# A graph's normalized input, turned by DMA in two 16-bit planes instead of by TensorE

## The chip, the core and the metric

The kernel runs on one core of one Trainium2 chip. The metric is the time of one execution on the device, in microseconds (us). The core has five engines that run side by side and wait for each other through semaphores: TensorE (PE, with its weight loads shown apart as PEld), VectorE (DVE), ScalarE (ACT), GpSimd (POOL) and SyncE (SP), which here only issues DMAs. Each engine works through its own queue in order. Matrix results land in PSUM[...]; everything else lives in SBUF, 128 partitions wide.

## The reference

There are 64 graphs of 256 nodes with 512 features each (`x` is 64 x 256 x 512, fp32) and an adjacency of 256 x 256 booleans for each. Two layers follow one another, and each adds its result to `x`:

```python
h = jnp.maximum(_layernorm(x, axis=-1), 0.0)
x = x + _L0_gnn_ref(h, adj, ...)   # 8 heads of 64
h = jnp.maximum(_layernorm(x, axis=-1), 0.0)
x = x + _L1_gnn_ref(h, adj, ...)   # 4 heads of 64
```

Layer 0 maps `h` with one matrix to `m`, takes queries and keys from `m`, forms softmax scores over 256 nodes and keeps those edges whose cosine between the heads of `m` is over 0.1, then mixes messages (`h` through another matrix) with them. Layer 1 is a plain masked attention over `h`. What matters here is the first step of layer 0: `h` is the layer norm of `x` with a ReLU behind it, and the products need it with the features on the partitions, so the 256 x 512 matrix of a graph has to be turned.

## The kernel before

All matrices are fp32. The features of a graph lie in tiles `[128, 4, 256]` (128 features on the partitions, four groups of them, 256 nodes); the nodes-first form `xs` is `[128, 2, 512]`. The products with 512 x 512 matrices are done in seven block products instead of eight (`seven_products`, lines 245 to 310), whose left factors `ss` come from GpSimd (`left_factors`, tile `sh`, line 235). `seven_products` is a generator: every `next` on it issues one piece, so pieces of several products stand between each other in the program.

The order of every engine's instructions is the order of the program (`manual_schedule`). The loop is `period(i)`, run for i = 0 to 64 (line 541 on). In one period four graphs are worked on at different stages:

- `b` = graph i-1: the rest of its layer 1 (scores `sc1`, mask, sums `zb`, values, the product `p_o` with the result, the store);
- `g` = graph i: layer 0's scores `sc0`, cosines `co`, edge selection, values, and its layer-1 input and projections `p_qk`, `p_v`;
- `nx` = graph i+1: layer 0's map `p_m`, messages `p_s`, queries `p_q`, keys `p_k`, norms;
- `n2` = graph i+2: its moments (mean and variance by `bn_stats`), the deviation, the normalized rows `xn`, and the turned input `hT`.

Graph i+3 is loaded in the period (lines 183 and 185), after the store of `b`, in whose buffer it lands.

For n2, before the change: `moments` on VectorE in the middle of the period (lines 193 to 196), `deviations` with the Sqrt on ScalarE next to g's own (line 199), `normalized` on VectorE (line 206: subtract the mean, multiply by 1/deviation), and at the end of the period `normal_input`, which is `turned` and `left_factors`. `turned` (lines 210 to 217) transposes each 128 x 128 block with a TensorE matmul against the identity (line 215, four for each half, tile `p_t`, one PSUM bank for each half) and lets ScalarE apply the ReLU while it moves the bank to `hT` (line 216). The same helper turns g's layer-1 input, tile name `hT` too.

Three other things share resources with the change:

- ScalarE has to load a table of functions before Sqrt and before Exp. A period does this once each: all Sqrt instructions stand together (lines 199 and 637), and a dummy Exp on `spare` (line 639) brings the Exp table back before the next scores.
- SyncE issues all DMAs of the loop: the `far` transposes (line 439, four in a period, 16-bit, 128x256), the `mask` transposes (line 324), the spread of the softmax sums through DRAM (`by_rz` line 358, `own` line 360), the spread of the norms (`by_rn`, `nT`), the store (646) and the loads.
- Tiles of a pool with one buffer are reused by tag. `kT` is written by `keys(nx)` and read by the next period's `sc0`; `nT` is written by `spread(nx)` near the end of a period and last read by the next period's cosines; `hT` of nx is read by its map and messages.

Of the kernel before, what the change touches and what calls it, by code (L numbers as in the profile page):

```python
# [8 lines left out]
F32 = mybir.dt.float32  # L9
BF16 = mybir.dt.bfloat16  # L10
I32 = mybir.dt.int32
U8 = mybir.dt.uint8
AF = mybir.ActivationFunctionType
ALU = mybir.AluOpType
AX = mybir.AxisListType
# [131 lines left out]
def fast_path(ctx, tc, a, w, chk, out):  # L147
# [4 lines left out]
    nc = tc.nc  # L152
    x, adj = a["x"], a["adj"]
    B, S, D = x.shape
    P, DH = 128, 64
# [17 lines left out]
    def bank(name, shape=(P, 2, S), dtype=F32):  # L173
        return ring.tile(list(shape), dtype, tag="bank", name=name)
# [14 lines left out]
    def moments(g, tag):  # L189
        st = small.tile([P, NT, 6], F32, tag="st", name=f"st{tag}")  # L190
        g.mv = small.tile([P, NT, 2], F32, tag="mv", name=f"mv{tag}")
        for t in range(NT):
            nc.vector.bn_stats(st[:, t, :], g.xs[:, t, :])  # L193
            nc.vector.bn_aggr(g.mv[:, t, :], st[:, t, :])
        g.rs = small.tile([P, NT], F32, tag="rs", name=f"rs{tag}")
        nc.vector.tensor_scalar_add(g.rs, g.mv[:, :, 1], LN_EPS)

    def deviations(g):
        nc.scalar.activation(g.rs, g.rs, AF.Sqrt)
        nc.vector.reciprocal(g.rs, g.rs)  # L200

    def normalized(g, tag):
        g.xn = []
        for t in range(NT):
            xn = sb2.tile([P, D], F32, tag="xn", name=f"xn{tag}_{t}")
            nc.vector.tensor_scalar(xn, g.xs[:, t, :], g.mv[:, t, 0:1], g.rs[:, t:t + 1],  # L206
                                    op0=ALU.subtract, op1=ALU.mult)
            g.xn.append(xn)
# [7 lines left out]
            nc.scalar.activation(hT[:, :, t * P:(t + 1) * P], p, AF.Relu)  # L216
        return hT

    def features_first(wt, src, ms, name):

        p = bank(name)
        nk = wt.shape[1]
        for n, m in enumerate(ms):
            for c in range(nk):
                nc.tensor.matmul(p[:, n, :], wt[:, c, m * P:(m + 1) * P], src[:, c, :],
                                 start=(c == 0), stop=(c == nk - 1))
        return p

# [210 lines left out]
    def far_added(g, c):  # L441
        if not g.last:
            nc.gpsimd.tensor_add(g.d[c], g.d[c], g.e[c][:, :, :S])  # L443
# [97 lines left out]
    def period(i):  # L541
        g = graphs.get(i) if i < B else None
        b, nx, n2 = graphs.get(i - 1), graphs.get(i + 1), graphs.get(i + 2)
        def off_edges(cs):
            for c in cs if g else ():
                masked(g.e[c], g.mask, edges=False)
                g.d[c] = halves(g.e[c], f"0_{i}_{c}")


        if b:  # L550
            b.e1 = [exps(products(b.k1T, b.q1T, c, f"sc1_{b.i}_{c}"), f"1_{b.i}_{c}") for c in range(NIC)]
            for c in range(NIC):
                masked(b.e1[c], b.mask, edges=True)
            if b.last:
                for t in range(NT):
                    values_in(b, t)
            else:
                b.d1 = [halves(b.e1[c], f"1_{b.i}_{c}") for c in range(NIC)]
        if nx:
            m, s = mapped(nx), messages(nx)  # L560
            next(m)
        if g:
            for c in range(NKC):
                g.e[c] = exps(products(g.kT, g.qT, c, f"sc0_{i}_{c}"), f"0_{i}_{c}")
        if nx:
            next(s)
        off_edges((0, 1))
        if nx:
            next(m)
        off_edges((2,))  # L570
        if nx:
            next(m)
            next(s)
            next(m)
            halved(nx)

        if g:
            for c in range(NKC):
                far_off(g, c, cosines(g, c))
                if c == 0:  # L580
                    off_edges((3,))
            for c in range(NKC):
                far_added(g, c)
        if nx:
            q = queries(nx)
            next(q)
            next(s)
            next(q)
            squares(nx)
            next(s)  # L590
        for c in range(NKC):
            if g:
                far_back(g, c)
            if nx and c < 3:
                next((q, s, q)[c])
        if nx:
            lengths(nx, norms(nx))

        if i == 0:
            w.finish_seven(w.wqk1)  # L600
        if b:
            sums1(b)
            values1(b)
        if n2:
            moments(n2, f"0_{n2.i}")
        if g:
            g.avs = sb1.tile([P, NKC, S], F32, tag="wide", name=f"avs{i}")
            g.sms = sb1.tile([P, S], F32, tag="sms", name=f"sms{i}")
            values(g, 0)
            values(g, 1)  # L610
            sums(g)
        if nx:
            k = keys(nx)
            next(k)
        if b:
            nc.scalar.activation(b.rz, b.rz, AF.Copy, accum_out=chk[:, b.i, 3:4])
        if g:
            sums_back(g)
            heads_back(g)
        if nx:  # L620
            next(k)
        if n2:
            edges(n2)
        if b:
            divided(b)
        if g:
            moments(g, f"1_{i}")
        if nx:
            next(k)
        if g:  # L630
            deviations(g)
        if n2:
            deviations(n2)
        if g:
            normalized(g, f"1_{i}")
        if nx:
            nc.scalar.activation(nx.rn, nx.rn, AF.Sqrt)

        nc.scalar.activation(spare[:, 1:], spare[:, :1], AF.Exp)
        if b:  # L640
            for t in range(NT):
                result(b, t)
                if b.last:
                    nc.sync.dma_start(out=out_t[b.i][:, t], in_=b.xs[:, t])
            if not b.last:
                nc.sync.dma_start(out=out_t[b.i], in_=b.xs)
        if i + 3 < B:
            graphs[i + 3] = load(i + 3)
        if g:
            g.h1T = turned(g, f"1_{i}", "wide")  # L650
            j = queries_keys1(g)
            for t in range(NT):
                nc.gpsimd.tensor_add(g.xs[:, t, :], g.xs[:, t, :], w.bo_b)
        if nx:
            next(k)
        if g:
            next(j)
        if nx:
            nc.vector.reciprocal(nx.rn, nx.rn)
            spread(nx)  # L660
        if g:
            next(j)
        if n2:
            normalized(n2, f"0_{n2.i}")
        if g:
            next(j)
            if not g.last:
                values_in(g, 0)
            next(j)
        if n2:  # L670
            normal_input(n2)
        if g and not g.last:
            values_in(g, 1)
        if nx:
            units(nx)
# [5 lines left out]
    with tc.manual_schedule():  # L681
        spare = small.tile([P, 2], F32, tag="spare", name="spare", bufs=1)
        nc.vector.memset(spare, 0.0)
        graphs = {0: load(0)}
        w.load_map()
        gws = [sb2.tile([P, 2, D], F32, tag="e", name=f"gw{k}", bufs=6) for k in range(2)]
        w.load_folded(gws)
        w.load_scores()
        graphs.update({n: load(n) for n in range(1, min(3, B))})
        w.load_rest()  # L690

        def normal(n):
            moments(graphs[n], f"0_{n}")
            deviations(graphs[n])
            normalized(graphs[n], f"0_{n}")

        g = graphs[0]
        normal(0)
        normal_input(g)
        edges(g)  # L700
        w.finish_seven(w.wm)
        m = mapped(g)
        next(m)
        next(m)
        w.fold(gws, bank, w.put_seven)
        next(m)
        w.finish_seven(w.wq)
        next(m)
        halved(g)
        squares(g)  # L710
        w.finish_seven(w.wk)
        q, k, s = queries(g), keys(g), messages(g)
        next(q)
        lengths(g, norms(g))
        w.fold_bias(sb2.tile([P, NKC, P], F32, tag="xn", name="gbb"), bank)
        w.finish_seven(w.wc)
        for step in (k, q, k, q, k, q, k):
            next(step)
        nc.scalar.activation(g.rn, g.rn, AF.Sqrt)
        nc.vector.reciprocal(g.rn, g.rn)  # L720
        spread(g)
        if B > 1:
            edges(graphs[1])
            normal(1)
        nc.scalar.activation(spare[:, 1:], spare[:, :1], AF.Exp)
        for _ in range(5):
            next(s)
        units(g)
        if B > 1:
            normal_input(graphs[1])  # L730
        for i in range(B + 1):
            period(i)

# [297 lines left out]
```

## Time and profile before

| | |
|---|---|
| median of 3 runs | 3752.13 us (3750.98 to 3752.83) |
| span of the profiled execution | 3750.8 us |
| one period in the middle | about 57.5 us |
| p_t transposes on TensorE (line 215) | 1024, 272 to 448 ns each as shown, overlapping |
| ReLU evictions of p_t (line 216) | 256, 595 ns each |
| xn on VectorE (line 206) | 256, 929 ns each |
| bn_stats on VectorE (line 193) | 256, 666 ns each |
| far transposes (line 439) and mask transposes (line 324) | 256 and 128, 1.21 and 1.23 us of SyncE each |

How to read it: an instruction's duration on TensorE is longer than its place in the queue, since matmuls overlap. The chain of waits followed back from the last instruction gives the place: each piece of it begins where the one before ends. "Idle before" an instruction is the time in which its engine did nothing, with the instruction it waited for. Time of DMA-issuing instructions is not counted as busy.

### The profile page before, as it was taken

How to read it: one execution, taken by the hardware profiler on the slowest of the kernel's cores; microseconds unless marked ns; L12 is line 12 of the kernel's file. 1: busy time of each engine (PE TensorE's matmuls, PEld its weight loads, DVE VectorE, ACT ScalarE, POOL GpSimd, SP SyncE). 2: the span in 40 equal slices, each digit the busy share in tenths (PEclk: the TensorE clock that was granted, in tenths of full speed). 3: DMA queues.
4: the chain of work that ended last, by engine and by line, in shares of the span. 5: the costliest groups of instructions: out<-in, count | busy, mean ns of one | idle time of the engine just before them, and what ended most of it. 6: DMA issues, size and time to landing. Idle time of an engine off the chain costs nothing.

```text
span 3750.8 us, 76663 instructions
## 1 busy us (share of the span) xinstructions
PE 3704.9 (99%) x29649; PEld 3145.3 (84%) x29649; DVE 2878.5 (77%) x5350; ACT 1587.8 (42%) x4108; POOL 2468.6 (66%) x2044
## 2 busy tenths in 40 slices
PE   7999999999999999999999999999999999999997
PEld 7888888888888888888888888888888888888885
DVE  6777777777777777777777777777777777777775
ACT  2444444444444444444444444444444444444443
POOL 3667666676676676676766766767667667666673
PEclk9999999999999999999999999999999999999999
DMA  3111111111111111111111111111111111111101
GB/s 101 39 39 41 48 32 48 48 29 47 45 35 48 33 46 48 32 46 45 33 48 39 41 48 32 48 48 29 47 45 34 48 33 47 48 32 46 46 26 35
DMA packets 226096, 159.23 MB, mean 42 GB/s; under 512 B 137536, under 2 KB 192064, under 8 KB 225728
## 3 DMA queue, kind: packets, MB, share of 16 engines
q1 hardware_dynamic: 223456, 154.22, 14.4%
q8 instruction: 238, 3.90, 0.4%
q14 instruction: 130, 1.06, 0.1%
q10 hardware_dynamic: 2272, 0.04, 0.0%
HBM read 94.67 MB, written 34.34 MB: 34 GB/s over the span
## 4 chain that ended last, share of the span: by engine, by line
PE 97%; DVE 1%; DMA 1%; POOL 0%; issue 0%; SPq 0%; ACT 0%; DVEq 0%; ACTq 0%; POOLq 0%
PE sc L386 9%; PE av L413 9%; PE p_q L261 6%; PE p_m L261 6%; PE p_k L261 6%; PE p_qk L261 6%; PE p_s L256 6%; PE p_o L538 6%; PE p_v L505 6%; PE p_q_z L261 5%; PE co L423 5%; PE p_qk_z L261 5%; PE p_m_z L261 5%; PE p_k_z L261 4%; PE p_s_z L256 4%; PE p_t L215 3%
## 5 line engine op out<-in xcount | busy, mean ns | idle before, releaser
L406 POOL TENSOR_TENSOR d<-e 128x512 f32<-128x512 f32 x382 | 721.0, 1913 | 34.5 <-DVE e L400 28.9
L402 DVE TENSOR_TENSOR e<-e,mask 128x1024 f32<-128x1024 f32 x256 | 456.9, 1805 | 64.2 <-ACT e L393 64.2
L239 POOL TENSOR_TENSOR sh<-hT 128x256 f32<-128x256 f32 x128 | 93.0, 726 | 585.6 <-ACT hT L216 585.6
L393 ACT ACTIVATE e<-sc 128x512 f32<-128x512 f32 x768 | 389.8, 620 | 143.3 <-PE sc L386 143.1
L491 POOL TENSOR_TENSOR xs<-xs,o 128x512 f32<-128x512 f32 x128 | 187.4, 1484 | 387.2 <-DVE o L489 387.2
L450 POOL TENSOR_TENSOR d<-d,e 128x512 f32<-128x512 f32 x252 | 321.0, 1274 | 171.7 <-DVE e L448 169.9
L443 POOL TENSOR_TENSOR d<-d,e 128x512 f32<-128x512 f32 x252 | 311.8, 1267 | 0.0
L436 DVE SCALAR_TENSOR_TENSOR e<-co,e 128x256 f32<-128x256 f32 (+1 forms) x1024 | 282.1, 343 | 35.8 <-ACT up L433 34.7
L216 ACT ACTIVATE hT<-p_t 128x512 f32<-128x512 f32 x256 | 139.2, 595 | 280.8 <-PE p_t L215 280.8
L538 PE MATMUL p_o<-wo,own 128*128 128x512 f32 x512 | 234.9, 602 | 9.6 <-DVE own L533 9.6
L505 PE MATMUL p_v<-wv,hT 128*128 128x256 f32 x1024 | 242.1, 379 | 0.0
L386 PE MATMUL sc<-qT,kT 64*128 64x256 f32 x2048 | 238.2, 382 | 0.0
L433 ACT ACTIVATE up<-co,below 128x128 bf16<-128x128 f32 x512 | 159.6, 366 | 183.0 <-PE co L423 177.3
L413 PE MATMUL av<-e,sem 128*64 128x256 f32 x2048 | 232.2, 379 | 0.9 <-DVE e L448 0.9
L448 DVE SCALAR_TENSOR_TENSOR e<-far,e 128x256 f32<-128x256 bf16 x256 | 230.5, 901 | 0.0
L206 DVE TENSOR_SCALAR xn<-xs,mv,rs 128x512 f32<-128x512 f32 x256 | 227.4, 929 | 0.1
L386 PEld LDWEIGHTS sc<-qT,kT 64*128 64x128 f32 x2048 | 192.9, 187 | 27.5
L413 PEld LDWEIGHTS av<-e,sem 128*64 128x64 f32 x2048 | 146.8, 137 | 75.6 <-DVE e L448 1.7
L505 PEld LDWEIGHTS p_v<-wv,hT 128*128 128x128 f32 x1024 | 184.7, 190 | 20.2 <-issue 0.3
L400 DVE SCALAR_TENSOR_TENSOR e<-mask,e 128x1024 f32<-128x1024 bf16 x128 | 184.8, 1482 | 21.8 <-ACT e L393 21.8
L193 DVE BATCH_NORM_STATS2 st<-xs 128x6 f32<-128x512 f32 x256 | 170.6, 666 | 24.8 <-POOL xs L491 21.7
L423 PE MATMUL co<-nT 64*128 64x256 f32 (+1 forms) x2048 | 184.9, 330 | 0.0
(194 smaller groups left out, 9008.8 us busy)
## 6 DMA issues: line engine op xcount, KB each, us to landing
xs<-in_x_dram SPq DMA_DIRECT2D x64, 512.0 KB
nT<-by_rn SPq DMA_DIRECT2D x128, 256.0 KB
out_dram<-xs SPq DMA_DIRECT2D x63, 512.0 KB
own<-by_rz SPq DMA_DIRECT2D x128, 128.0 KB
ad<-in_adj_dram SPq DMA_DIRECT2D x64, 64.0 KB
far<-up SPq DMA_TRANSPOSE x256
mask<-adb SPq DMA_TRANSPOSE x128
wm<-in_L_gnn_map_w_dram SPq DMA_DIRECT2D x4, 256.0 KB
```

The source lines that it names most:

```text
L256: nc.tensor.matmul(region, src[:, c, :], wt[:, block, c, :], start=p not in opened, stop=True, skip_group_check=True)
L261: nc.tensor.matmul(region[:, f, :], wt[:, block, c, f * P:(f + 1) * P], src[:, c, :], start=p not in opened, stop=True, skip_group_check=True)
L386: nc.tensor.matmul(ps[s][:, j, :], rows[h, c, j * P:(j + 1) * P], cols[h, c, :], start=True, stop=True)
L393: nc.scalar.activation(e[:, s, :], p.rearrange("p j q -> p (j q)"), AF.Exp, scale=SCALE)
L402: nc.vector.tensor_mul(e, e, m)
L406: nc.gpsimd.tensor_add(d, e[:, :, :S], e[:, :, S:])
L413: nc.tensor.matmul(av[s * DH:(s + 1) * DH, n, :], vs[:, j, (h0 + s) * DH:(h0 + s + 1) * DH], q[:, s, j * S:(j + 1) * S], start=(j == 0), s ...
L423: nc.tensor.matmul(ps[s][:, j, j * P:], g.nT[h, c, j * P:(j + 1) * P], g.nT[h, c, j * P:], start=(j == 0), stop=True, skip_group_check=True)
L443: nc.gpsimd.tensor_add(g.d[c], g.d[c], g.e[c][:, :, :S])
L450: nc.gpsimd.tensor_add(g.d[c], g.d[c], g.e[c][:, :, S:])
L505: nc.tensor.matmul(g.p_v[:, t, :], g.h1T[:, c, t * P:(t + 1) * P], w.wv1[:, c, :], start=(c == 0), stop=(c == NKC - 1))
L538: nc.tensor.matmul(p, b.avs1[:, c, t * P:(t + 1) * P], w.wo1[:, c, :], start=(c == 0), stop=(c == NIC - 1))
```

## The change

For graphs 2 to 63 the input of layer 0 is no longer turned on TensorE. ScalarE normalizes it and applies the ReLU in one instruction (scale 1/deviation, bias -mean/deviation). The DMA transpose turns 16-bit elements, so each fp32 word is seen as two 16-bit halves: ScalarE copies the low halves and the high halves apart into `flat` (nodes first), SyncE issues a DMA transpose for each half and each half of the nodes into `turn`, and ScalarE puts the halves back together in `hT` (`join`, once for each plane).

```diff
+    def shifts(g, tag):
+
+        deviations(g)
+        g.shift = small.tile([P, NT], F32, tag="shift", name=f"shift{tag}")
+        nc.vector.scalar_tensor_tensor(g.shift, g.mv[:, :, 0], -1.0, g.rs, op0=ALU.mult, op1=ALU.mult)
+        g.flat = sb1.tile([P, NT, 2, D], U16, tag="kT", name=f"flat{tag}")
+        g.turn = sb1.tile([P, 2, NKC, S], U16, tag="nT", name=f"turn{tag}")
+
+    def sent(g, tag, t):
+
+        xn = sb2.tile([P, D], F32, tag="xn", name=f"xn{tag}_{t}")
+        nc.scalar.activation(xn, g.xs[:, t, :], AF.Relu, bias=g.shift[:, t:t + 1], scale=g.rs[:, t:t + 1])
+        bits = xn.bitcast(U16).rearrange("p (d k) -> p k d", k=2)
+        for k in range(2):
+            nc.scalar.copy(g.flat[:, t, k, :], bits[:, k, :])
+            nc.sync.dma_start_transpose(out=g.turn[:, k, :, t * P:(t + 1) * P], in_=g.flat[:, t, k, :])
+
+    def joined(g, tag):
+        g.hT = sb1.tile([P, NKC, S], F32, tag="hT", name=f"hT{tag}")
+        g.bits = g.hT.bitcast(U16).rearrange("p c (q k) -> p k c q", k=2)
+
+    def join(g, k):
+        nc.scalar.copy(g.bits[:, k], g.turn[:, k])
```

The pieces go into the period at these places (a helper `features_first` that nothing calls is dropped as well):

```diff
             for c in range(NKC):
                 far_added(g, c)
+        if n2:
+            shifts(n2, f"0_{n2.i}")
         if nx:
             q = queries(nx)
             next(q)
             next(s)
+        if n2:
+            sent(n2, f"0_{n2.i}", 0)
+        if nx:
             next(q)
             squares(nx)
             next(s)
+        if n2:
+            sent(n2, f"0_{n2.i}", 1)
...
-        if n2:
-            moments(n2, f"0_{n2.i}")
...
             sums(g)
+        if n2:
+            joined(n2, f"0_{n2.i}")
+            join(n2, 0)
...
             heads_back(g)
+        if n2:
+            join(n2, 1)
...
-        if n2:
-            deviations(n2)
...
-        if n2:
-            normalized(n2, f"0_{n2.i}")
...
         if n2:
-            normal_input(n2)
+            n2.left_h = left_factors(n2.hT, "sh", n2.i)
+        if i + 3 < B:
+            moments(graphs[i + 3], f"0_{i + 3}")
```

The moments are now taken one period earlier, at the end of the period in which the graph is loaded, since the deviation is needed in the middle of the next one; for graph 2 they are taken ahead of the loop. `flat` uses the buffer of `kT` and `turn` that of `nT`, in the part of the period in which those are not in use. Graphs 0 and 1 are still turned on TensorE ahead of the loop.

More of the change, by code (lines that the diff above doesn't have):

```diff
@@ L12 @@
 U8 = mybir.dt.uint8
+U16 = mybir.dt.uint16
 AF = mybir.ActivationFunctionType
@@ L217, in turned @@
         return hT
[L219 to L227, printed above, removed]
+    def shifts(g, tag):
[16 more added lines that the diff above has]
+        nc.scalar.copy(g.bits[:, k], g.turn[:, k])
     HC = NKC // 2
@@ L730, in fast_path @@
             normal_input(graphs[1])
+        if B > 2:
+            moments(graphs[2], "0_2")
         for i in range(B + 1):
```

## The prediction

> **What bounds the kernel now.** I first read the page's busy shares and the chain that ended last, to see which engine sets the end:
>
> ```profile
> PE 3704.9 (99%) x29649; PEld 3145.3 (84%) x29649; DVE 2878.5 (77%) x5350; ACT 1587.8 (42%) x4108; POOL 2468.6 (66%) x2044
> PE 97%; DVE 1%; DMA 1%; POOL 0%; issue 0%; SPq 0%; ACT 0%; DVEq 0%; ACTq 0%; POOLq 0%
> ```
>
> TensorE is busy 99% of the span, and 97% of the chain is TensorE work following TensorE work. So an instruction taken off TensorE shortens the kernel by its place in that chain, as long as nothing else becomes late. Next I read the chain in order of time through one period in the middle (pieces: start us, us, what), where the transposes stand:
>
> ```profile
> 1829.37 0.88 PE p_t L215 x8
> 1830.25 0.89 PE p_k_z L261 x8
> ...
> 1838.23 0.89 PE p_qk_z L261 x8
> 1839.12 0.87 PE p_t L215 x8
> 1839.99 1.73 PE p_v L505 x8
> ...
> 1886.83 0.87 PE p_t L215 x8
> ```
>
> There are two groups of eight transposes in a period. The first (1829.37) turns g's layer-1 input and stays; the second (1839.12, between the last p_qk_z and the second half of p_v) is `normal_input(n2)` and goes. It costs 0.87 us of unbroken chain. The period is 1886.83 - 1829.37 = 57.46 us, and its 50 pieces join without a hole, so TensorE has no idle time into which a late input could fall. Every new wait of TensorE therefore costs in full, and what matters is the slack of the other engines where the new work lands. ScalarE takes nearly all of it, so I read its timeline over a period (start, us, work, in brackets the idle time before):
>
> ```profile
> 1856.56 2.59 ACT L433 ACTIVATE up<-co,below 128x128 bf16<-128x128 f32 x8 [2.81 <-PE co L423]
> 1860.56 0.62 ACT L278 ACTIVATE u2p_q<-p_q,bq 128x128 f32<-128x128 f32 x2 [1.41 <-issue]
> ...
> 1865.84 0.62 ACT L278 ACTIVATE u5p_q<-p_q,bq 128x128 f32<-128x128 f32 x2 [4.14 <-PE p_q L261]
> 1866.36 1.15 ACT L334 ACTIVATE sq<-mT 128x512 f32<-128x512 f32 x2
> 1870.48 0.38 ACT L528 ACTIVATE rz<-zb 128x256 f32<-128x256 f32 x1 [2.97 <-PE zb L524]
> ...
> 1878.76 0.62 ACT L278 ACTIVATE u2p_k<-p_k,bk 128x128 f32<-128x128 f32 x2 [1.48 <-PE p_k L261]
> ...
> 1882.53 0.62 ACT L278 ACTIVATE u5p_k<-p_k,bk 128x128 f32<-128x128 f32 x2 [2.04 <-PE p_k L261]
> ```
>
> The holes of 1.41, 4.14, 2.97, 1.48 and 2.04 us are where the change puts its work. The new transfers go to the one queue of SyncE, so its timeline comes last:
>
> ```profile
> 1857.21 6.05 SPq L439 DMA_TRANSPOSE far<-up  x4
> 1874.98 0.56 SPq L358 DMA_DIRECT2D by_rz<-rz  x1
> 1876.69 1.25 SPq L360 DMA_DIRECT2D own<-by_rz  x2
> ```
>
> Between the end of the far transposes, 1863.26, and by_rz at 1874.98 the queue has 11.7 us free.
>
> **What the Trainium skill says.** "ScalarE: Activation LUTs", What ACT_TABLE_LOAD costs, prices an ACTIVATE at 186 ns + 0.833 ns per element, 93 ns more per [128,1] operand, 93 ns of overlap back to back; 512 elements come to 612 ns, and the trace's avs eviction of 128x512 takes 597, so I use it. The same section gives a table load 1283 ns, as the trace does (1283), and about 1380 ns of drain. The trace has no drain: a load starts at 1883.17 and the next ACTIVATE at 1884.51. Its section Table sets says that relu, copy and identity are in every set; the trace agrees, since in the prologue Relu, Identity, Copy and Square run between the Sqrt load at 5.44 and the Exp load at 52.81 with no load between. "DMA: Bandwidth & Descriptors", DMA Transpose (X-bar), allows 2-byte elements only, hence two planes, and wants transposes of two streams kept apart; here all are issued by SyncE, as far and mask are already.
>
> **The change part by part.**
> *Off TensorE*: eight transposes, 0.87 us, for graphs 2 to 63 (0 and 1 are still turned on TensorE): 62 x 0.87 = 53.9 us, on the path. *Off ScalarE*: two p_t evictions of 0.6 us in each period. *Off VectorE*: `normalized(n2)`, 2.63 us for the pair at 1891.72; both were beside TensorE.
>
> *Sqrt earlier.* `shifts` puts n2's Sqrt behind the last up (ends 1859.15), with the table load that used to stand at 1883.17: 1.28 + 0.20 gives 1860.65, when u2p_q now starts at 1860.56. The later Sqrts find the table loaded, so loads move but do not multiply. Cost nothing: the 1.41 us hole hides all but 0.1, and the reader of u2p_q, the qT add at 1864.07, is far off. On VectorE the reciprocal and the shift queue behind the last far_off product, which ends at 1863.02: by 0.22 (reciprocals) and 0.17 (the nearest 128x2 row) to 1863.4. The sem and qT adds behind them slip by 0.4 and are caught up in VectorE's idle 2.16 us before 1866.65, so TensorE's next z product does not see it.
>
> *sent(0).* xn with two operands is 186 + 427 + 186 = 0.80 us, each strided 16-bit copy 0.61 less 0.09. From 1863.4: 1864.2, 1864.7, 1865.2. u5p_q starts at 1865.84: fits with 0.6 spare. *sent(1)* follows sq (1867.51): 1868.2, 1868.7, 1869.25; rz comes at 1870.48: 1.2 spare. *join(0)* behind the sms read (1877.29), 186 + 853 = 1.04 us, ends at 1878.3, before u2p_k at 1878.76. *join(1)* behind the rc read (1880.49) ends at 1881.5, before u5p_k at 1882.53. The trace shows no 16-bit strided copy; the bounds are this price and twice it. With twice, sent(0) ends at 1866.3 and join(0) at 1879.4; u5p_q and u2p_k start 0.5 and 0.65 late, but VectorE reads them at 1867.78 and 1880.82 only, after they have ended (1866.9, 1880.0). Cost nothing at both ends.
>
> *Transfers.* A 128x256 transpose holds SyncE 1.21 us (median of 256 far issues); for the mask at 1883.94 its 256 packets of 256 B run at 1885.13 to 1885.53 and the last 4 B completion packet ends at 1885.93. The new ones are 128x512; issue lies between 1.2 and 2.4 us (same and double). I take 2.4: starts at 1864.7, 1867.1, 1869.5, 1872.0, end 1874.4, still before by_rz at 1874.98, and landed by about 1875.6 (0.8 us of packets, 0.4 to completion). join(0) looks at 1877.3. Cost nothing. What queues behind the last one is by_rz, and own (needed by VectorE at 1881.16, landed 1879.76) behind that.
>
> *Slots.* flat takes the slot of kT, free from the end of the sc0 products (1849.3) to the first kT add (1880.82); turn that of nT, free from the cosines' end (1858.5) to the nT spread at about 1894; hT's last reader before join(0) is p_s_z at 1868.4. None binds.
>
> *moments.* Two bn pairs leave the middle and go to the period's end, for a graph loaded in the same period. Its load's packets end at 1894.1; VectorE is free for moments from the last qk add, 1897.36, and has 1.85 us idle before v at 1899.21. The work is 1.77 us (0.86 for each half). As TensorE's p_v comes 0.87 earlier, v may wait up to 0.9 us; its reader and that of nT behind it are over 10 us away, and p_v's bank is wanted again only by the sc0 products some 4 us on. Cost nothing.
>
> *Start.* In period 0 the moments at 93.85 stand between the wqk sums and r on the chain, 1.8 us; they move to the prologue, where VectorE has 3.97 us idle before 64.70. I count 1.3.
>
> Sum: 53.9 + 1.3 = 55.2; 3752.1 - 55.2 = **3697 us**.
>
> **The rivals.**
> *Hidden work shows (about 3725).* TensorE waits for one of the tight spots, most likely the load of graph i+3 landing late and holding VectorE at moments, or a late join(0). For it: spares of 0.4 to 0.9 us, in a period that shrinks by 0.87. Against: for each the next reader has slack of its own. Half the saving lost is 27 us.
> *The queue takes the place of the transposes (about 3800, slower).* If a 128x512 transpose held SyncE 3.6 us, three times the 128x256, four from 1864.7 end at 1879.1, by_rz is 4.1 late, own lands at 1883.9, VectorE's division starts 2.8 us late, and p_o, which has 1.2 us of slack (division over at 1882.2, p_o at 1883.39), waits 1.6. Net 0.75 lost in each period, 62 x 0.75 = 46. For it: by_rz stands right behind the transposes. Against: it needs more than proportional growth.
> *More than its own time (about 3680).* TensorE's remaining waits, such as p_q_z on the VectorE add uup_q (18.1 us over the kernel), go as well: 53.9 + 18. Against: that add is queued behind far_back, which stays.
>
> **How the numbers follow.** Forecast 0.76, half lost 0.11, slower 0.10, more 0.03. Faster: 0.76 + 0.03 and nearly all of the half-lost case (0.09); same 0.02; slower 0.10. The range holds the forecast and most of the half-lost case: 3687 (10 us under) to 3735. It leaves out the slow rival, the tail of the half-lost case and the biggest gain, some 0.17.
>
> **What would show it.** Right: p_t of 512 + 16 instructions where there were 1024, a period of 56.6 us in the chain with p_v directly behind p_qk_z, ScalarE near 50% busy (about 4.9 us more in a period), TensorE still 97% or more of the chain, by_rz issued as soon as rz's reciprocal is over. Wrong: transposes of flat holding SyncE over 2.5 us, TensorE waiting for own, for kT or for u2p_k, more than one Sqrt table load in a period, or VectorE waiting for xs at moments with TensorE waiting behind it.

## The result and the profile after

The changed kernel takes 3698.84 us (median of 4 runs, 3697.64 to 3699.82) against 3751.56 us before on the same chip: ratio 0.986, 95% interval 0.9843 to 0.9877. It is 52.7 us faster; the prediction said 55, to 3697. The two profiled executions, single ones, lie 55.0 us apart (spans of 3750.8 and 3695.8 us).

The page of the kernel after, the busy shares and the chain by engine:

```profile
PE 3651.0 (99%) x29153; PEld 3091.7 (84%) x29153; DVE 2774.1 (75%) x5288; ACT 1904.1 (52%) x4480; POOL 2348.0 (64%) x2044
PE 96%; DVE 1%; DMA 1%; POOL 0%; issue 0%; ACT 0%; SPq 0%; DVEq 0%; ACTq 0%; POOLq 0%
```

TensorE has 496 instructions less, which is 62 x 8, and is still 96% of the chain. ScalarE went from 1587.8 to 1904.1 us busy, 5.1 us more in each of 62 periods, without a place in the chain. The chain in order of time over a period in the middle (start us, us, piece):

```profile
1827.48 2.82 PE co L438 x32
...
1865.76 1.73 PE p_v L520 x8
1867.49 0.89 PE p_qk_z L276 x8
1868.38 1.73 PE p_v L520 x8
...
1884.06 2.82 PE co L438 x32
```

Between p_qk_z and the second p_v nothing is left of the eight transposes, and the period is 1884.06 - 1827.48 = 56.58 us instead of 57.46. ScalarE's timeline shows where its new work lies (start, us, work, idle before in brackets):

```profile
1830.97 1.28 ACT L200 ACT_TABLE_LOAD   x1
1832.27 0.21 ACT L200 ACTIVATE rs<-rs 128x2 f32<-128x2 f32 x1
...
1836.02 0.81 ACT L231 ACTIVATE xn<-xs,shift,rs 128x512 f32<-128x512 f32 x1 [2.51 <-POOL d L458]
1836.87 1.14 ACT L234 COPY flat<-xn 128x512 uint16<-128x512 uint16 x2
1837.91 0.62 ACT L293 ACTIVATE u5p_q<-p_q,bq 128x128 f32<-128x128 f32 x2
...
1848.99 1.34 ACT L242 COPY hT<-turn 128x1024 uint16<-128x1024 uint16 x1
1850.57 0.63 ACT L293 ACTIVATE u2p_k<-p_k,bk 128x128 f32<-128x128 f32 x2 [0.24 <-PE p_k L276]
...
1852.18 1.36 ACT L242 COPY hT<-turn 128x1024 uint16<-128x1024 uint16 x1
1854.34 0.63 ACT L293 ACTIVATE u5p_k<-p_k,bk 128x128 f32<-128x128 f32 x2 [0.79 <-PE p_k L276]
```

The 4.14 us hole ahead of u5p_q is closed to nothing: u5p_q follows the flat copies without idle time. Ahead of u2p_k 0.24 of 1.48 us are left, ahead of u5p_k 0.79 of 2.04. Before xn stand 2.51 us of idle time put down to GpSimd. The forecast had about 1.7 of them (u4p_q over at 1861.7, xn at 1863.4); the other 0.8 it did not have. xn reads the shift, and the timelines of VectorE and, last line, GpSimd show why that is late:

```profile
1834.75 0.15 DVE L201 RECIPROCAL rs<-rs 128x2 f32<-128x2 f32 x1
1834.93 1.01 DVE L224 SCALAR_TENSOR_TENSOR shift<-mv,rs 128x2 f32<-128x2 f32 x1
1835.86 0.41 DVE L301 TENSOR_TENSOR sem<-p_s_z,u2p_s 128x256 f32<-128x256 f32 x1
...
1834.66 1.26 POOL L458 TENSOR_TENSOR d<-d,e 128x512 f32<-128x512 f32 x1
```

The shift has two numbers in each partition and takes 1.01 us, seven times the reciprocal in front of it. It ends at 1834.93 + 1.01 = 1835.94; the GpSimd addition to d (line 458) that was under way ends at 1834.66 + 1.26 = 1835.92. The kernel before shows the same on a larger instruction, far_back, whose two tensors both come from SBUF (two lines of VectorE, then one of GpSimd):

```profile
1867.45 0.41 DVE L448 SCALAR_TENSOR_TENSOR e<-far,e 128x256 f32<-128x256 bf16 x1
1868.57 0.98 DVE L448 SCALAR_TENSOR_TENSOR e<-far,e 128x256 f32<-128x256 bf16 x1
...
1868.01 1.27 POOL L450 TENSOR_TENSOR d<-d,e 128x512 f32<-128x512 f32 x1 [1.44 <-DVE e L448]
```

With GpSimd idle it takes 0.41 us, beside GpSimd's addition 0.98. So the wait could be read from the trace before the change. The timeline of SyncE's queue:

```profile
1837.51 5.93 SPq L235 DMA_TRANSPOSE turn<-flat  x4
1846.79 0.57 SPq L373 DMA_DIRECT2D by_rz<-rz  x1
```

The four transposes end at 1843.44, and by_rz leaves when the reciprocal of rz is over (1846.76).

### The profile page after: what moved, and what is told of

Its sections match the earlier page's. It is cut to its first block, busy times and chain, and to the rows that moved or that the text cites. A ratio compares the mean times of both kernels' runs of the same rounds, so it can differ in the third digit from the quotient of the medians.

```text
span 3695.8 us, 76415 instructions
## 1 busy us (share of the span) xinstructions
PE 3651.0 (99%) x29153; PEld 3091.7 (84%) x29153; DVE 2774.1 (75%) x5288; ACT 1904.1 (52%) x4480; POOL 2348.0 (64%) x2044
## 4 chain that ended last, share of the span: by engine, by line
PE 96%; DVE 1%; DMA 1%; POOL 0%; issue 0%; ACT 0%; SPq 0%; DVEq 0%; ACTq 0%; POOLq 0%
PE sc L401 9%; PE av L428 9%; PE p_k L276 6%; PE p_q L276 6%; PE p_m L276 6%; PE p_qk L276 6%; PE p_s L271 6%; PE p_o L553 6%; PE p_v L520 6%; PE p_q_z L276 5%; PE co L438 5%; PE p_qk_z L276 5%; PE p_k_z L276 5%; PE p_m_z L276 5%; PE p_s_z L271 4%; PE sm L481 2%
## 5 line engine op out<-in xcount | busy, mean ns | idle before, releaser
L417 DVE TENSOR_TENSOR e<-e,mask 128x1024 f32<-128x1024 f32 x256 | 465.0, 1836 | 55.0 <-ACT e L408 55.0
L491 DVE RECIPROCAL r<-rt 128x16 f32<-128x16 f32 x64 | 16.5, 258 | 253.3 <-PE rt L489 253.3
L553 PEld LDWEIGHTS p_o<-wo,own 128*128 128x128 f32 x512 | 93.6, 193 | 104.7 <-issue 101.7
L231 ACT ACTIVATE xn<-xs,shift,rs 128x512 f32<-128x512 f32 x124 | 100.5, 810 | 156.1 <-POOL d L458 153.6
```

The source lines that it names most:

```text
L417: nc.vector.tensor_mul(e, e, m)
L553: nc.tensor.matmul(p, b.avs1[:, c, t * P:(t + 1) * P], w.wo1[:, c, :], start=(c == 0), stop=(c == NIC - 1))
```

## The experiments

Each kernel was timed beside the kernel before on its own chip, so ratios are compared: 0.986 is the kernel after.

### e1: the transposes off, nothing in their place

```diff
 # the kernel before
-            normal_input(n2)
+            n2.hT = sb1.tile([P, NKC, S], F32, tag="hT", ...)
+            for t, xn in enumerate(n2.xn):
+                nc.scalar.activation(n2.hT[:, :, t * P:(t + 1) * P], xn.rearrange("p (c q) -> p c q", q=P), AF.Relu)
+            n2.left_h = left_factors(n2.hT, "sh", n2.i)
```

> The kernel before, without the eight TensorE transposes of n2: ScalarE writes hT for graphs 2 to 63 straight from the unturned rows, so their layer-0 input holds the wrong order of values; everything else stays as before, and no DMA turns anything. It is the most that taking the transposes off can bring. Theory (the gain is the transposes' place on TensorE, 62 x 0.87 us, and the new work is hidden): about 3698 us, within 3 us of the kernel after. Rival A (the new work costs something, and the kernel after has lost a part of a larger gain): clearly under 3695. Rival B (part of the gain comes from VectorE, relieved of xn): clearly over 3702, since VectorE still does xn here.

3695.97 us, ratio 0.9857 (0.9842 to 0.9872), the same as the kernel after within both intervals. A period in the middle, from one start of the cosines to the next, is as long as in the kernel after, 1882.96 - 1826.38 = 56.58 us:

```profile
1826.38 2.82 PE co L423 x32
...
1882.96 2.82 PE co L423 x32
```

So the DMA route costs nothing that the intervals or the chain can tell: the change brings all that taking eight transposes off can bring. Rival B (VectorE's relief gave a part) falls as well, as VectorE makes xn here.

### e2: the transposes back, beside the DMA route

```diff
 # the kernel after
         if n2:
+            for t in range(NT):
+                p = bank(f"p_t0_{n2.i}_{t}", [P, NKC, P])
+                for c in range(NKC):
+                    nc.tensor.transpose(p[:, c, :], n2.xs[:, t, c * P:(c + 1) * P], w.ident)
             n2.left_h = left_factors(n2.hT, "sh", n2.i)
```

> The kernel after with eight TensorE transposes put back at their old place, into banks that nobody reads; the DMA route stays and feeds hT. Theory: TensorE gets 0.87 us in each of 62 periods, 3699 + 54 = 3753 us, as before the change. Rival B (VectorE's relief gave a part): less than 3748, because that relief stays. Rival A (the new work is late by some tenths somewhere): less than 3748 too, since the longer period would hide it.

Ratio 0.9998 (0.999 to 1.0007): the gain is gone, within an interval of some 3 us on either side. Its chain in order of time holds the transposes (here line 695) at the length they had before:

```profile
1833.86 0.89 PE p_qk_z L276 x8
1834.75 0.87 PE p_t L695 x8
1835.62 1.73 PE p_v L520 x8
```

### e3: VectorE relieved, the transposes kept

```diff
 # the kernel before
-            normalized(n2, f"0_{n2.i}")
+            n2.shift = ...   # -mean/deviation, on VectorE
+            for t in range(NT):
+                nc.scalar.activation(xn, n2.xs[:, t, :], AF.Relu, bias=n2.shift[:, t:t + 1], scale=n2.rs[:, t:t + 1])
...
-            moments(n2, f"0_{n2.i}")
...
             normal_input(n2)
+        if i + 3 < B:
+            moments(graphs[i + 3], f"0_{i + 3}")
```

> The kernel before with only the other half of the change: xn of n2 is made on ScalarE instead of VectorE (at its old place in the period) and the moments are taken one period earlier, at the period's end; the transposes stay on TensorE. Theory: VectorE and ScalarE are beside the path, so only period 0 gains (moments off the chain there, 1 to 2 us): 3750 us. Rival B (VectorE's relief is worth something in each period): 3740 or less. If the moments at the period's end hold up TensorE: over 3753.

Ratio 1.0003 (0.9994 to 1.0011), no change. VectorE's busy time fell from 2878.5 to 2802.6 us and moved nothing. Period 0 did gain: from the first p_m of period 0 to that of period 1 the chain has 114.72 - 58.29 = 56.43 us here and 119.30 - 60.41 = 58.89 before. That is 2.5 us, too little for ratios that can't tell less than some 3 us.

### e4: every 16-bit copy twice

```diff
 # the kernel after
-            nc.scalar.copy(g.flat[:, t, k, :], bits[:, k, :])
+            for _ in range(2):
+                nc.scalar.copy(g.flat[:, t, k, :], bits[:, k, :])
...
-        nc.scalar.copy(g.bits[:, k], g.turn[:, k])
+        for _ in range(2):
+            nc.scalar.copy(g.bits[:, k], g.turn[:, k])
```

> The kernel after with each of the four flat copies and both joins done twice by ScalarE: 4 x 0.52 + 2 x 1.34 = 4.8 us more in each period. Theory (ScalarE's holes, and the slack of those who read its results, take twice the work, as the prediction had it): 3699 us, no change, with u5p_q, u2p_k and u5p_k starting about 1 us later each. Rival A (ScalarE is at its limit in these places): TensorE waits for uup_q, kT or uup_k, 0.3 to 1 us in each period, 3718 to 3760.

3711.46 us, ratio 0.9902 (0.9887 to 0.9917): 0.0042 over the kernel after, about 16 us, so the expectation missed. (The medians, taken on two chips, lie 12.6 us apart; this is the "12 us" of the next expectation.) In the chain a period from one start of the cosines to the next is mostly 56.87 us instead of 56.58, which makes 18 us in 62 periods. The chain of this kernel leaves TensorE once in a period:

```profile
1839.66 1.24 POOL d L460
1840.90 0.09 issue
1840.99 0.82 ACT xn L231
...
1843.65 0.62 ACT flat L235
1844.27 0.54 ACT u5p_q L295 x2
1844.81 0.02 issue
1844.83 0.43 DVE uup_q L323
1845.27 0.04 issue
1845.31 1.16 PE p_q_z L278 x8
```

From the end: TensorE's last p_q_z waits for VectorE's add uup_q, this for u5p_q, this for the doubled copies, these for xn, and xn for the GpSimd addition behind which the shift was held. TensorE waits for uup_q in 61 periods, 11.1 us in all. Here only the flat copies matter; the doubled joins, ahead of u2p_k and u5p_k, do not appear in the chain of this period. Whether the late start or the length of the copies is to blame, this run can't say.

### e5: the same with a shift that does not wait

```diff
 # e4
-        nc.vector.scalar_tensor_tensor(g.shift, g.mv[:, :, 0], -1.0, g.rs, op0=ALU.mult, op1=ALU.mult)
+        for t in range(NT):
+            nc.vector.tensor_scalar(g.shift[:, t:t + 1], g.mv[:, t, 0:1], g.rs[:, t:t + 1], -1.0,
+                                    op0=ALU.mult, op1=ALU.mult)
```

> The kernel of the doubled copies, with the shift made by two VectorE instructions with one tensor input each (mean, times 1/deviation as a per-partition number, times -1) instead of one with two tensor inputs. In the kernel after, that 128x2 instruction took 1.01 us, since it ran while GpSimd was in its additions to d, and xn began only when GpSimd's last one ended. Theory (the 12 us that doubled copies cost come from this late shift; ScalarE's holes would otherwise take the double work): shift over 0.7 us earlier, TensorE's wait for uup_q gone, 3698 to 3702 us. Rival (the doubled copies themselves are too long, whenever they start): 3711 us again. Rival (an instruction with one tensor input waits for GpSimd as well): shift again ends with GpSimd's addition, 3711 us.

3699.2 us, ratio 0.9859 (0.9844 to 0.9874): the loss of e4 is gone with the double copies still there, and most periods are 56.58 us again. The instructions of the shift (minimum, median, maximum in ns):

```profile
L225 DVE TENSOR_SCALAR shift<-mv,rs x124: 202/208/215, 80.7 to 3535.7; 128x1 f32<-128x1 f32 x124
```

Against those of the kernel after:

```profile
L224 DVE SCALAR_TENSOR_TENSOR shift<-mv,rs x62: 999/1009/1027, 81.6 to 3532.8; 128x2 f32<-128x2 f32 x62
```

Two instructions of 0.21 us ran while GpSimd was in the same additions; one pair and the addition around it:

```profile
1834.46 0.33 DVE L225 TENSOR_SCALAR shift<-mv,rs 128x1 f32<-128x1 f32 x2
...
1834.18 1.29 POOL L462 TENSOR_TENSOR d<-d,e 128x512 f32<-128x512 f32 x1
```

So the form with two tensor inputs in SBUF waits for GpSimd, and this small one with one does not. The operation as such is not to blame: e<-co,e is a SCALAR_TENSOR_TENSOR too, with one of its inputs in PSUM, and takes 0.43 us at the most in the kernel after, where twelve of them run in 3.25 us from 1831.57 on beside GpSimd's work. Nor is one tensor input a guard for every size: in the kernel before, xn on VectorE (128x512, one tensor input) took 0.54 us each at 1885.38, where GpSimd was idle, and 1.22 and 1.49 us at 1891.72, beside two GpSimd additions (1891.39 to 1894.07).

The late start alone (the kernel after) costs nothing that e1 can tell, nor do the double copies alone as far as the ratio of e5 can tell; together they cost the loss of e4. (Some periods of e5 are 0.1 to 1.4 us longer than 56.58; in one of them, near 1850 us, the doubled joins lie in the chain.)

### e6, e9 and e7: more on SyncE's queue

```diff
 # the kernel after; e6 has range(1), e7 range(2)
             sent(n2, f"0_{n2.i}", 1)
+            spill = sb1.tile([P, NT, S], U16, tag="adb", name=f"spill{n2.i}")
+            for _ in range(1):
+                for t in range(NT):
+                    for k in range(2):
+                        nc.sync.dma_start_transpose(out=spill[:, :, t * P:(t + 1) * P], in_=n2.flat[:, t, k, :S])
```

> The kernel after with four more DMA transposes of 128x256 behind the four of flat on SyncE's queue in each of 62 periods, into a tile that nobody reads. Theory: each holds SyncE 1.21 us, the last ends at about 1848.4 on the clock of the period that ends its flat transposes at 1843.4, so by_rz is 1.6 us late and own lands 1.6 us late, but VectorE's division is still over 0.8 us ahead of p_o: no change, 3699 us. Rival (the queue is at its limit already): TensorE waits for own up to 1.6 us in each period, up to 3798 us.

3967.88 us, ratio 1.0569: a miss by 270 us. The two transposes of one t write one place, so the queue waited for a landing within each pair (152.4 us in all, put down to "DMA spill<-flat"):

```profile
2029.50 5.93 SPq L235 DMA_TRANSPOSE turn<-flat  x4
2035.53 8.45 SPq L617 DMA_TRANSPOSE spill<-flat  x4
2044.08 0.57 SPq L373 DMA_DIRECT2D by_rz<-rz  x1
```

by_rz left 10.3 us after the start of zb (2033.77 in the chain), where the kernel after needs 5.0 (1841.79 to 1846.79): 5.3 us late. TensorE's timeline at p_o in three periods:

```profile
526.43 5.37 PE L553 MATMUL p_o<-wo,own 128*128 128x512 f32 x8 [1.98 <-DVE own L548]
1988.82 5.22 PE L553 MATMUL p_o<-wo,own 128*128 128x512 f32 x8 [3.50 <-DVE own L548]
2174.67 3.67 PE L553 MATMUL p_o<-wo,own 128*128 128x512 f32 x8 [2.62 <-DVE own L548]
```

And the busy time and granted clock (PEclk) of four stretches: before the wait and behind it at 1988.82, then a slow p_o and one at full speed:

```profile
core 0: us, PE busy (x) PEld busy (x) DVE busy (x) ACT busy (x) POOL busy (x), PEclk, DMA share, GB/s
1975.00:1982.00 7.00, 7.00 (x72) 5.31 (x69) 2.96 (x6) 4.05 (x9) 1.28 (x1) 1.00 0.12 26
1988.00:1992.00 4.00, 3.18 (x4) 1.52 (x5) 3.82 (x11) 1.46 (x3) 0.00 (x0) 0.57 0.08 18
...
526.43:531.80 5.37, 5.37 (x10) 2.30 (x11) 3.99 (x11) 2.00 (x4) 0.00 (x0) 0.68 0.06 12
827.10:830.77 3.67, 3.67 (x10) 1.70 (x11) 3.49 (x11) 1.94 (x4) 0.00 (x0) 1.00 0.08 18
```

At 1988.82 p_o waits 3.50 us for own, and after the wait the clock is at 0.57, so that p_o takes 5.22 us. At full clock it takes 3.44 us of the chain without a wait in front of it and 3.67 behind one. Not every p_o is slow: of the 59 between 200 and 3830 us in the chain, 47 are, by some 2 us each. The waits come to 173.0 us, where the kernel after has 9.8, and the slow p_o to about 47 x 2 = 94 us, an estimate; 163 + 94 make 257 of the 269 us of growth. "TensorE: Matmul & The Clock Gate" in the Trainium skill, Part 1, says that the clock halves after an idle window of about 3.4 us. In this trace shorter waits are enough: 1.98 us at 526.43 brought a slow p_o, while 2.62 us at 2174.67 did not. Each of the 59 behind 2.65 us or more is slow and none behind less than 1.98 is; in between it goes both ways.

The next run takes the pairs apart: 128x128 each, into four places of the tile.

```diff
+            spill = sb1.tile([P, 4, P], U16, tag="adb", name=f"spill{n2.i}")
...
+                        nc.sync.dma_start_transpose(out=spill[:, 2 * t + k, :], in_=n2.flat[:, t, k, :P])
```

> Four extra DMA transposes behind those of flat again, each of 128x128 into a part of its own of the unread tile. In the run before with four, each pair wrote one place, so the queue waited for landings and the four held SyncE 8.6 us instead of 4.9. Theory (SyncE has 3.3 us free there and TensorE's p_o another 1.2 us or so of slack behind own; a transpose holds SyncE 1.2 us whatever its size): the four take 4.8 us, by_rz is about 1.6 us late, own's division about 0.5 to 1 us late, no time lost: 3699 us. Rival (what costs is the extra transposes as such, landing or issuing beside the others): over 3800 us, as before.

3745.63 us, ratio 0.9988 (0.9982 to 0.9995): 47 us over the kernel after. A miss too, but a much smaller loss than e6's, so waits between the pairs were most of that one. SyncE's timeline in this kernel:

```profile
1981.51 5.00 SPq L616 DMA_TRANSPOSE spill<-flat  x4
1986.61 0.57 SPq L373 DMA_DIRECT2D by_rz<-rz  x1
```

by_rz left 8.06 us after zb (1978.55), 3.1 us late instead of 1.6: turn's four had taken 7.13 us here instead of 5.93. In the chain own lands at 1991.84, 13.3 us after zb, and in the kernel after 9.85; p_o starts 14.2 us after zb where it was 13.4. So 3.5 us of delay lost 0.8 us in this period. Over the kernel TensorE waits 44.3 us for own instead of 9.8, and p_o takes 3.67 us of the chain instead of 3.44: 34.5 + 62 x 0.23 make 49 us, near the 47 measured. Some 2.7 us of delay behind by_rz cost nothing, and the queue, which was free for 3.35 us in front of by_rz, was overspent by four transposes. The mean clock did not fall (0.996).

> The same with eight more transposes, about what the slower rival of the prediction was: SyncE is held until about 1853.3, by_rz and own are 6.5 us late, VectorE divides at about 1858.2 to 1859.3 where TensorE wanted p_o at 1855.2: TensorE loses about 4.1 us in each period, 62 x 4.1 = 254 us, about 3953 us, with waits of p_o for own. Rival (transposes on the queue don't hold up what stands behind them): 3699 us.

4461.83 us, ratio 1.1897: slower by far more than expected, so it can't serve as a measure of the queue alone. Its eight transposes held SyncE 14.3 us (again waiting for each other), and as they read flat, the first kT add waited for the buffer: TensorE's p_k_z lost 411.8 us to kT, p_o 150.7 us to own, and the mean clock fell to 0.92.

### e8: VectorE's add ahead of far_back

```diff
 # the kernel after
         for c in range(NKC):
-            if g:
-                far_back(g, c)
             if nx and c < 3:
                 next((q, s, q)[c])
+            if g:
+                far_back(g, c)
```

> The kernel after with VectorE's order changed in the part of the edges that come back: each piece of queries and messages is issued ahead of far_back of the same number instead of behind it, so the add uup_q no longer stands behind a far_back product (0.33 us). In the chain of the kernel after, the last p_q_z piece takes 1.04 us where the others take 0.89. Theory: that 0.15 us goes in each of 63 periods, 9 us, about 3690 us, since TensorE's waits now lie on its path in full. Rival (far_back, now later, holds up the values products av instead): 3699 or more.

3687.35 us (3684.84 to 3687.61), ratio 0.9828 (0.9814 to 0.9841), the fastest of all. The last p_q_z of a period in its chain (start, us, piece), and below it that of the kernel after:

```profile
1830.40 0.94 PE p_q_z L276 x8
...
1840.17 1.04 PE p_q_z L276 x8
```

The period, from one start of the cosines to the next, is 1874.18 - 1817.71 = 56.47 us instead of 56.58; 0.11 x 63 makes 7 us. The ratios are 0.0032 apart, 12 us, with intervals of 5 us on either side; the profile of this run also began its first period 5.5 us earlier than that of the kernel after (first p_m at 56.55 instead of 62.06), ahead of the loop, which the edit does not touch. From that first p_m to the end it takes 3684.0 - 56.55 = 3627.5 us, the kernel after 3695.8 - 62.06 = 3633.7, so 6.3 us less. So some 7 us are the edit's, shown by the chain, and the rest is open.

## Why the prediction was right, and where its steps were not

**The path.** The saving is the place of eight transposes in TensorE's chain: 62 x 0.87 us. e1 takes it with nothing in its place and e2 gives it back, so this is shown. That VectorE's relief is worth nothing in a period is shown by e3. One reading was off without a consequence: the period's chain has 40 pieces; 50 is the count of the whole window that was read.

**Sqrt earlier.** As foretold: one table load of 1.28 us behind the last up, the Sqrt over 0.1 us after u2p_q would have started, no second Sqrt load in the period.

**sent(0).** The step that was mis-sized is the shift: 0.17 us were taken from the nearest 128x2 row, an instruction with one tensor input; with two inputs, both in SBUF, it took 1.01. The rest fits its price: xn 0.81 (0.80), a flat copy 0.616 (0.61). So sent(0) had no spare where 0.6 were foretold. In the kernel after this costs nothing that e1 can tell.

**Twice the copies cost nothing.** Wrong, by 16 to 18 us (e4), and wrong through the shift (e5 has the double copies without the loss). With single copies the slack of the add uup_q took the late shift; the forecast had spent the same slack on the second copies.

**join.** 1.35 us instead of 1.04; its spares were 0.24 and 0.79 instead of 0.4 and 1.0. Still hidden, and nearly so when doubled (e5).

**Transfers.** The upper bound was taken, 2.4 us of SyncE for each; it is 1.26, hardly more than the 1.21 of half the size. The slow rival (3.6 us) was far off in its premise. Its law is right in kind: delay of by_rz passes to p_o less the slack behind it. But it put that slack at 2.5 us (4.1 late, 1.6 lost), where e9 has about 2.7, and it left out that such a wait can slow the clock as well, which added some 2 us in 47 of 59 periods of e6.

**moments.** At the period's end they hold up nothing (e3). In period 0 they gave 2.5 us instead of 1.3. In the profile after, the work ahead of period 0 was 1.65 us longer (first p_m at 62.06 instead of 60.41), though the change adds nothing to TensorE there; among the profiles that were read at this place it came between 56.5 and 62.1, so a single profile can't show 2 us. From the first p_m to the end the kernel after is 3690.4 - 3633.7 = 56.7 us shorter, which is 62 x 0.87 + 2.5 within 0.3. That the measured time came within 2 us of the forecast is in part chance: in the two profiles a gain that was sized 1.2 us too low met a start that was 1.65 us later. Where the 2 us between the forecast and the median lie, the runs leave open.

**The rival with more than its own time.** It said that the wait for uup_q could go too, and was set aside as that add stands behind far_back. e8 moves it ahead, and two thirds of the piece's excess go: the reason given was the right one.

## What to carry to other kernels

Where one engine fills its chain without a hole, an instruction moved off it is worth its place in the chain. The work that takes over is free as long as it stays within the slack of those who read its results, so count that slack and not only the hole that the work lies in. Count slack along the whole chain of small instructions that start the new work: a two-element one was the tight link here, and the queue of the one DMA-issuing engine came next, as four more transposes on it already cost 47 us. Ahead of that, look in the chain for pieces that are longer than their like: the order of VectorE's instructions was worth some 7 us more (e8).

## What the runs showed of the hardware that was not expected

- A VectorE instruction with two tensor inputs in SBUF, of two elements, took 1.01 us beside GpSimd's additions and ended with the one under way; in e3, where it mostly stands beside GpSimd's additions of bo_b, it took 0.15 at the least and 0.95 as the median. The 128x256 far_back took 0.41 with GpSimd idle and 0.98 beside an addition (before). With one tensor input the shift took 0.21 beside the same additions (e5), and the reciprocal 0.15, but xn of 128x512 took 1.22 to 1.49 instead of 0.54 (before). "VectorE: DVE Perf Modes" in the Trainium skill, Two Vector instructions with no wait between them, says that a second SBUF read interface is shared with GpSimd, and that an instruction with two SBUF tensor inputs reads through it, and one with a single input too in a two-port mode. The runs agree with that as a cause and did not test it by itself; whether xn ran in such a mode they do not show.
- A DMA transpose held SyncE 1.23 us for 128x128, 1.21 for 128x256 and 1.26 for 128x512 (medians of e9, before and after): among these sizes the size hardly counts.
- A wait of TensorE slowed its clock: to 0.57 in the 4 us around the end of a 3.50 us wait, to 0.68 over the p_o behind one of 1.98 us (e6). Behind a wait of 2.62 us p_o still ran at full speed, so the length of the wait alone does not settle it below 2.65 us. With waits that were mostly 0.2 to 0.9 us (e9) the mean clock stayed at 0.996.
- A ScalarE copy of 16-bit halves took 0.616 us for 512 elements read with a gap between them, the price that the prediction used, but 1.35 us for 1024 elements written with a gap, 0.31 over that price.
